# Attention: the first three score bursts of a batch moved beside the last three mixings of the batch in front of it, and added sums later in a slot

## The chip, the cores and the metric

The kernel runs on one core of one Trainium2 chip. Its time is the device time of one execution in microseconds (us). The kernel before took 1703.79 us (median of three runs, 1703.03 to 1704.57). Engines are named as the profile names them: PE multiplies matrices (PEld loads its weights), DVE is the vector engine, ACT the scalar engine, POOL the GpSimd engine, and SP the queue that starts most transfers.

## The reference, cut to what matters

The network has four layers on x of 8 batches, 512 positions and 256 columns: a state-space layer, a mixture of experts, attention and a second mixture of experts. Each layer is added to x and takes a layer norm of x as its input.

```python
def _L0_attn_b_ref(x, Wqkv, Wout):              # H = 16 heads of 16 columns
    qkv = jnp.einsum('btd,ed->bte', x, Wqkv)    # then cut into q, k, v by head
    scores = jnp.einsum('bhtd,bhsd->bhts', q, k) * SCALE
    scores = jnp.clip(scores, -10.0, 10.0)
    mask = jnp.triu(jnp.full((t, t), NEG), k=1)
    attn = jax.nn.softmax(scores + mask[None, None, :, :], axis=-1)
    out = jnp.einsum('bhts,bhsd->bhtd', attn, v)
    return jnp.einsum('btd,ed->bte', out.transpose(0, 2, 1, 3).reshape(b, t, d), Wout)

x = x + _L0_attn_a_ref(_layernorm(x), ...)      # state space
x = x + _L0_ffn_ref(_layernorm(x), ...)         # 16 routed experts, 4 for each token, and 2 shared ones
x = x + _L0_attn_b_ref(_layernorm(x), ...)
x = x + _L0_ffn_ref(_layernorm(x), ...)
```

## The kernel before

The work is done in stretches. The first holds the state-space layer. Then the routed experts of the first mixture run, which end near 722 us. The attention stage follows up to about 1190 us, and the routed experts of the second mixture are last. The change touches the attention stage, and lines below are those of the kernel before.

**A slot.** The attention stage runs over the eight batches. In slot b several pieces of work are issued beside each other: `main(b)`, the attention of batch b; `project(b + 1)`, the queries, keys and values of the next batch; the shared experts of batch b-2 (from slot 2 on); the routing of batch b-1 (norm, logits, choices) and the sends of rows of batch b-2 to their experts; and the loading and norm of x of batch b+2.

**How x arrives.** Each mixture's routed experts leave their results in two parts in memory. `load_sum` (L154) starts two transfers on SP for batch b+2, `more` from one part (L157) and x from the other (L158), and later DVE adds them in two steps of 128 x 512 numbers (L165). These two steps are kept where the program puts them in DVE's order. The statistics (L443, L444), the reciprocal deviation (L462, with a step of POOL at L463) and the normed rows (L468) of that batch follow.

**Projections.** `project` computes four results of 512 columns, pq_0_0, pq_0_1, pq_1_0 and pq_1_1 (first number: a half of the heads; second: queries or keys), each by PE at L1190 into a bank of a pool of four. Queries are copied by ACT (L1198). Keys are copied twice, by ACT (L1200) and by DVE (L1201), each time with every second head set to zero. Two results of values (pv, L1208) follow.

**Bursts and mixings.** `main` splits the scores of a half of the heads into five bursts, so that a batch has ten, named here 0_0 to 0_4 and 1_0 to 1_4. A burst (`weights`, L1228) is a group of score matmuls (L1238) into two banks of a pool that holds just two tiles of that size ("pair"), two exponentials on ACT (L1248, about 1.02 us each), and on DVE two pairs of clamps (L1258, L1259), which also apply the causal mask. Because scores can be clamped as well after the exponential, the limits are those of the exponential. A mixing (`mix`, L1264) multiplies the weights of a burst into the values (L1274). It stands LAG = 3 bursts behind its burst. After a half of the heads is mixed, `share` (L1286) turns the result, divides it by its sum and puts it into oT (L1289 to L1299); then the output projection (`add_projection`, L485) and the add to x (L494) end the batch.

`made` holds the weights of bursts, as pieces of a ring of ten tiles. The ring of queries and keys has six tiles. A column is what one matmul step costs in the pieces' own count.

**What sets the order.** `beside` (L348) issues steps of several pieces, always from the one that has done the smallest share of its columns; `timed` (L364) gives steps of a piece places in the slot between 0 and 1. A planner behind it then moves instructions within each engine's order, by its own costs, but keeps what is marked to stay. Each engine then takes its instructions in the order that comes out, and waits on semaphores.

In slots 2 to 6 (`close`), a burst and the mixing three bursts behind are issued as one step; in slots 0, 1 and 7 they are two steps.

Of the kernel before, what the change touches and what calls it, by code (L numbers as in the profile page):

```python
# [18 lines left out]
B, T, D = 8, 512, 256  # L19
NT = T // P  # L20
KD = D // P
# [57 lines left out]
LAG = 3  # L79
# [3 lines left out]
def tile_hybrid_block(  # L83
# [31 lines left out]
    def bank(shape, name: str, kind: str = "one"):  # L115
        kind = instead.get(kind, kind)
        return stage[kind].tile(shape, FP, tag=kind, name=name)
# [1044 lines left out]
    class Attention:  # L1162
        mixture, ahead, copies, turns = 1, 2, by_both, (0.65, 0.85)
        early = 2
        norms, scores, choose = (0.0, 0.12, 0.2, 0.28), (0.29, 0.45, 0.55, 0.6), (0.66, 0.95)
        last_rows, last_scores = (0.2, 0.28), (0.35, 0.38)

        def end(self):
            for e in range(first_expert, E):
# [5 lines left out]
        def project(self, b: int, xnT):  # L1175
            tag = f"a{b}"

            q_sb = spot("qk", NO)
            k_sb = [spot("qk", NO) for _ in range(2)]


            v_sb = values(f"v_{tag}").rearrange("p (t c) -> p t c", t=NT)

            def steps():
                nc.gpsimd.memset(v_sb, 1.0)
                for o in range(NO):
                    for which in range(2):
                        pq = bank([P, T], f"pq_{tag}_{o}_{which}")
                        for k in range(KD):
                            nc.tensor.matmul(  # L1190
                                pq,
                                lhsT=wqkv_sb[:, k, which * D + o * P : which * D + (o + 1) * P],
                                rhs=xnT[:, k, :],
                                start=(k == 0),
                                stop=(k == KD - 1),
                            )
                        if which == 0:
                            nc.scalar.copy(q_sb[:, o, :], pq)  # L1198
                        else:
                            nc.scalar.mul(k_sb[0][:, o, :], pq, parity[:, 0:1])  # L1200
                            nc.vector.tensor_scalar(k_sb[1][:, o, :], pq, parity[:, 1:2], None, ALU.mult)  # L1201
                        yield KD * T
                for h in range(2):
                    pv = bank([P, 2, D], f"pv_{tag}_{h}")
                    for j in range(2):
                        t = 2 * h + j
                        for k in range(KD):
                            nc.tensor.matmul(  # L1208
                                pv[:, j, :],
                                lhsT=xnT[:, k, t * P : (t + 1) * P],  # L1210
                                rhs=wqkv_sb[:, k, 2 * D : 3 * D],
                                start=(k == 0),
                                stop=(k == KD - 1),
                            )
                        nc.scalar.copy(
                            v_sb[:, t, 0 : H * VC].rearrange("p (h c) -> p h c", c=VC)[:, :, 0:DK],
                            pv[:, j, :].rearrange("p (h c) -> p h c", c=DK),
                        )
                        yield KD * D

            return (q_sb, k_sb, v_sb), Piece(2 * NO * KD * T + NT * KD * D, steps())

        def main(self, b: int, made):
            q_sb, k_sb, v_sb = made
            tag = f"a{b}"
            held = {}

            def weights(o: int, i: int, at):  # L1228


                ps = [bank([P, 2, T], f"ps_{tag}_{o}_{i}_{two}", "pair") for two in range(2)]
                es = [spot("es", 2) for _ in range(2)]
                col = 0
                for w, c in BANKS[i]:
                    n = T - c * P
                    for j in range(HG):
                        r = slice(32 * j, 32 * j + 32)
                        nc.tensor.matmul(  # L1238
                            ps[j // 2][:, j % 2, col : col + n],
                            lhsT=k_sb[w][r, o, c * P : (c + 1) * P],  # L1240
                            rhs=q_sb[r, o, c * P : T],
                            start=True,
                            stop=True,
                        )
                        at[w, c, j] = es[j // 2][:, j % 2, col : col + n]
                    col += n
                for two in range(2):
                    nc.scalar.activation(es[two], ps[two], AF.Exp, scale=ATT_SCALE)  # L1248
                    if len({w for w, _ in BANKS[i]}) > 1:
                        each = es[two].rearrange("p j (w q) -> p (j w) q", w=2)  # L1250
                        diagonal, full = each[:, :, 0:P], each[:, :, P:]
                        limit = causal[:, 0, :].unsqueeze(1).to_broadcast([P, 4, P])
                    else:
                        mixed = len(BANKS[i]) * P
                        diagonal, full = es[two][:, :, 0:mixed], es[two][:, :, mixed:]
                        limit = causal[:, 0 : len(BANKS[i]), :].rearrange("p c q -> p (c q)")
                        limit = limit.unsqueeze(1).to_broadcast([P, 2, mixed])
                    nc.vector.scalar_tensor_tensor(diagonal, diagonal, LOW, limit, ALU.max, ALU.min)  # L1258
                    nc.vector.tensor_scalar(full, full, LOW, TOP, ALU.max, ALU.min)  # L1259
                return len(BANKS[i]) * T  # L1260

            order = [key for keys in MIXES for key in keys]

            def mix(o: int, i: int, at):  # L1264


                ended = []
                for w, c in MIXES[i]:
                    places = [c for which, c in order if which == w]
                    if c == places[0]:  # L1270
                        at["po", w] = bank([P, T], f"po_{tag}_{o}_{w}")
                    for j in range(HG):
                        h = 8 * o + 2 * j + w
                        nc.tensor.matmul(  # L1274
                            at["po", w][32 * j : 32 * j + 32, c * P : T],
                            lhsT=v_sb[:, c, h * VC : h * VC + 32],
                            rhs=at[w, c, j],
                            start=(c == places[0]),
                            stop=(c == places[-1]),
                            tile_position=(0, 32 * j),  # L1280
                        )
                    if c == places[-1]:
                        ended.append(w)
                return len(MIXES[i]) * T, ended
# [15 lines left out]

            def steps():
                held["oT"] = work.tile([P, NO, T], FP, tag="kb4", name=f"oT_{tag}", bufs=KB)
                made = [{} for _ in range(NO)]
                bursts = [(o, i, made[o]) for o in range(NO) for i in range(len(BANKS))]

                close = 1 < b < B - 1
                for n in range(len(bursts) + LAG):
                    columns, ended = 0, []
                    if n < len(bursts):
                        columns = weights(*bursts[n])  # L1310
                        if n >= LAG and not close:
                            yield columns
                            columns = 0
                    if n >= LAG:
                        o, i, at = bursts[n - LAG]
                        more, ended = mix(o, i, at)
                        columns += more
                    yield columns
                    for w in ended:
                        share(o, w, at)  # L1320
                        yield 0
                yield from add_projection(b, lambda c: held["oT"][:, c, :], wo_sb, KD, tag)

            return Piece(2 * NO * 2 * NT * T + NT * KD * D, steps())


    ready = {}
# [47 lines left out]
    def stretch(layer):  # L1375
# [5 lines left out]
        def norm(b: int, first: bool = False):  # L1381
            def place():
                xn[b] = kb4(f"xn_{i}_{b}")
                return xn[b]

            return normed(b, f"l{i}_{b}", place, first, first)
# [52 lines left out]
        for b in range(1 if begun else 0, B):  # L1439
# [38 lines left out]
            if nxt < B:  # L1478
                added = layer.load(nxt)
                if added is not None:  # L1480
                    pieces.append(timed(added, 0.24, 0.28))
                pieces += [
                    timed(norm(nxt), *spread(0.32, 0.44, NT), *spread(0.56, 0.64, NT)),
                    timed(turn(nxt), *layer.turns),
                ]
            issue(beside(*pieces))
# [128 lines left out]
```

## Time and profile before

| what | us |
|---|---|
| median of three runs | 1703.79 |
| profiled execution | 1640.85 |
| its span | 1638.8 |
| PE busy in the span | 1572.8 (96%) |
| DVE busy | 1154.8 (70%) |
| ACT busy | 744.7 (45%) |
| POOL busy | 759.1 (46%) |
| PE busy / DVE busy, 828.2 to 888.9 us (slot 2) | 59.23 / 50.60 of 60.7 |

The profile is of one execution, with its time beside it; its span starts with the first and ends with the last instruction, and all places in us count from the span's start. A row of groups gives the line, the engine, the operation, what it writes and reads, the number of instructions, their busy time and the mean of one in ns, and the engine's idle time just before them with what ended it. A row of waits says which instruction an engine stood at, what released it, and how long in sum, how often, and at most. Durations of neighbouring instructions on one engine overlap a little in the records, by about 0.08 us, so that a sequence is shorter than the sum of its durations.

### The profile page before, as it was taken

How to read it: one execution, taken by the hardware profiler on the slowest of the kernel's cores; microseconds unless marked ns; L12 is line 12 of the kernel's file. 1: busy time of each engine (PE TensorE's matmuls, PEld its weight loads, DVE VectorE, ACT ScalarE, POOL GpSimd, SP SyncE). 2: the span in 40 equal slices, each digit the busy share in tenths (PEclk: the TensorE clock that was granted, in tenths of full speed). 3: DMA queues.
4: the chain of work that ended last, by engine and by line, in shares of the span. 5: the costliest groups of instructions: out<-in, count | busy, mean ns of one | idle time of the engine just before them, and what ended most of it. 6: DMA issues, size and time to landing. Idle time of an engine off the chain costs nothing.

```text
span 1638.8 us, 34229 instructions
## 1 busy us (share of the span) xinstructions
PE 1572.8 (96%) x9992; PEld 1156.9 (71%) x9992; DVE 1154.8 (70%) x3623; ACT 744.7 (45%) x1461; POOL 759.1 (46%) x655
## 2 busy tenths in 40 slices
PE   5999998999999999999899999999999999999996
PEld 2566665589999999974344445355458999999995
DVE  7988887546677666637887977977864666666664
ACT  3322332145555555545544444444314555555553
POOL 3265665635556555540022422422553555555554
PEclk8999999999999999999999999999999999999998
DMA  5355422557777766641324324332654777777776
GB/s 169 108 179 185 159 87 98 204 95 107 124 125 106 102 101 98 90 75 40 91 77 131 94 85 128 86 98 82 228 173 93 108 123 111 131 137 138 129 140 131
DMA packets 281646, 195.31 MB, mean 119 GB/s; under 512 B 168593, under 2 KB 262065, under 8 KB 281457
## 3 DMA queue, kind: packets, MB, share of 16 engines
q1 hardware_dynamic: 228368, 119.40, 28.8%
q0 software_dynamic: 51984, 72.09, 24.6%
q8 instruction: 85, 1.39, 0.4%
q10 hardware_dynamic: 1104, 1.57, 0.3%
q14 instruction: 105, 0.85, 0.2%
HBM read 89.71 MB, written 103.23 MB: 118 GB/s over the span
## 4 chain that ended last, share of the span: by engine, by line
PE 33%; DVE 11%; DMA 6%; issue 1%; ACT 1%; SPq 1%; POOL 1%; DVEq 0%; POOLq 0%; ACTq 0%
PE ph L993 12%; PE pyr L1024 6%; DMA part<-rows 4%; PE pg_m L1107 3%; PE pd_m L1136 3%; PE ps_a L1238 2%; DVE w_all L1258 2%; PE po_a L1274 2%; DVE w_all L1259 1%; PE py_a L485 1%; DMA x<-part 1%; PE pv_a L1208 1%; PE pq_a L1190 1%; ACT w_all L1248 1%; PE pt L975 1%
## 5 line engine op out<-in xcount | busy, mean ns | idle before, releaser
L1034 POOL DMA_INDIRECT part<-rows x272 | 426.8, 1569 | 339.4 <-ACT rows L1033 238.4
L758 POOL DMA_INDIRECT xg<-sorted_m,slots_m x256 | 257.9, 1007 | 244.3 <-issue 76.8
L993 PEld LDWEIGHTS ph<-rows,gate 128*128 128x128 f32 x2160 | 277.8, 191 | 33.4 <-ACT rows L976 23.2
L993 PE MATMUL ph<-rows,gate 128*128 128x128 f32 x2160 | 291.5, 278 | 1.8 <-ACT rows L976 1.8
L993 PE MATMUL ph<-rows,up 128*128 128x128 f32 x2160 | 285.3, 275 | 0.0
L1024 PE MATMUL pyr<-w_all,rows 128*128 x1088 | 279.2, 380 | 0.0
L966 DVE COPY up<-w_all 128x512 f32 x270 | 118.7, 441 | 211.9 <-PE ph L993 196.6
L993 PEld LDWEIGHTS ph<-rows,up 128*128 128x128 f32 x2160 | 262.9, 192 | 0.0
L966 ACT COPY gate<-w_all 128x512 f32 x270 | 166.5, 618 | 122.0 <-PE ph L993 116.3
L1024 PEld LDWEIGHTS pyr<-w_all,rows 128*128 128x128 f32 x1088 | 186.8, 192 | 14.3
L1248 ACT ACTIVATE w_all<-ps_a 128x1024 f32<-128x1024 f32 x160 | 155.1, 1021 | 69.8 <-PE ps_a L1238 59.8
L1033 ACT ACTIVATE rows<-pyr,gain 128x256 f32<-128x256 f32 x272 | 128.9, 474 | 80.9 <-PE pyr L1024 63.7
L1001 ACT ACTIVATE rows<-ph 128x256 f32<-128x256 f32 x272 | 104.6, 384 | 114.6 <-PE ph L993 99.7
L1003 DVE TENSOR_TENSOR rows<-ph,rows 128x256 f32<-128x256 f32 x272 | 115.0, 423 | 31.7 <-ACT rows L1001 31.6
L1004 DVE TENSOR_TENSOR rows<-ph,rows 128x256 f32<-128x256 f32 x272 | 115.2, 424 | 26.2 <-PE pt L975 0.9
L1107 PE MATMUL pg_m<-xT_m,su_sb 128*128 128x512 f32 x256 | 123.9, 605 | 0.0
L1136 PE MATMUL pd_m<-sd_sb,act_m 128*128 128x256 f32 x512 | 121.2, 382 | 1.3 <-DVE sig_m L1122 1.1
L1107 PE MATMUL pg_m<-xT_m,sg_sb 128*128 128x512 f32 x256 | 122.2, 600 | 0.0
L1238 PE MATMUL ps_a<-w_all 32*128 32x384 f32 (+3 forms) x1024 | 106.9, 473 | 8.7 <-ACT w_all L1248 8.6
L1136 PEld LDWEIGHTS pd_m<-sd_sb,act_m 128*128 128x128 f32 x512 | 95.8, 190 | 22.9 <-issue 7.0
L1258 DVE SCALAR_TENSOR_TENSOR w_all<-w_all,causal 128x512 f32<-128x512 f32 (+1 forms) x160 | 92.1, 575 | 17.9 <-ACT w_all L1248 17.5
L1238 PEld LDWEIGHTS ps_a<-w_all 32*128 32x128 f32 x1024 | 46.7, 188 | 68.6 <-ACT w_all L1248 43.6
(213 smaller groups left out, 1954.8 us busy)
## 6 DMA issues: line engine op xcount, KB each, us to landing
rows<-xg SPq DMA_DIRECT2D x720, 32.0 KB
rows<-xg SPq DMA_DIRECT2D x92, 134.0 KB
part<-x SPq DMA_DIRECT2D x16, 512.0 KB
part<-ys_m SPq DMA_DIRECT2D x14, 512.0 KB
sum<-part SPq DMA_DIRECT2D x14, 512.0 KB
w_all<-in_L_ffn_gate_w_dram SPq DMA_DIRECT2D x27, 256.0 KB
w_all<-in_L_ffn_up_w_dram SPq DMA_DIRECT2D x27, 256.0 KB
w_all<-in_L_ffn_down_w_dram SPq DMA_DIRECT2D x27, 256.0 KB
```

The source lines that it names most:

```text
L758: nc.gpsimd.indirect_dma_start(out=xg[i], out_offset=bass.IndirectOffsetOnAxis(ap=slots[:, at : at + 1], axis=0), in_=rows[:, t, :], in_of ...
L966: copy(here, w_all[:, bass.ds(held[n][0] + half * KD * F, KD * F)])
L993: nc.tensor.matmul(ph[s][:, f * P : (f + 1) * P], lhsT=both[s][:, k * F + f * P : k * F + (f + 1) * P], rhs=rows[:, ROW + k * P : ROW + (k ...
L1004: made = nc.vector.tensor_mul(act, ph[1], act)
L1024: nc.tensor.matmul(py, lhsT=act[:, f * P : (f + 1) * P], rhs=w_all[:, bass.ds(w + 2 * KD * F + f * D, D)], start=(f == 0), stop=(f == KF - 1),
L1033: nc.scalar.mul(y, py, gain[:, TK : TK + 1])
L1034: acc = nc.gpsimd.indirect_dma_start(out=parts[i][n % 2], out_offset=bass.IndirectOffsetOnAxis(ap=rows[:, D + 2 * TK : D + 2 * TK + 1].bit ...
L1107: made = nc.tensor.matmul(dst, lhsT=w[:, k, f * P : (f + 1) * P], rhs=xnT[:, k, :], start=(k == 0), stop=(k == KD - 1),)
L1136: nc.tensor.matmul(py[:, j, :], lhsT=acts[n][:, f, t * P : (t + 1) * P], rhs=shared[n][3][:, f, :], start=(n == 0 and f == 0), stop=(n == ...
L1238: nc.tensor.matmul(ps[j // 2][:, j % 2, col : col + n], lhsT=k_sb[w][r, o, c * P : (c + 1) * P], rhs=q_sb[r, o, c * P : T], start=True, st ...
L1248: nc.scalar.activation(es[two], ps[two], AF.Exp, scale=ATT_SCALE)
L1258: nc.vector.scalar_tensor_tensor(diagonal, diagonal, LOW, limit, ALU.max, ALU.min)
```

## The change

It has two parts.

1. The bursts of a batch are made known when it is projected (`bursts`, `parts`). `weights` takes the batch as an argument. The main work of batch b now goes over the ten mixings of b. Beside mixing n stands burst n + 3 of b, and beside the last three mixings stand the first three bursts of b+1. In slot 0 the first three bursts of batch 0 come ahead, so that slot 0 has thirteen bursts, slots 1 to 6 ten and slot 7 seven. A burst and a mixing are one step in every slot, so `close` goes. The piece's column count is corrected for slots 0 and 7.
2. The two steps of L165 stand at 0.31 and 0.34 of a slot, where they stood at 0.24 and 0.28. The statistics of that batch are spread from 0.36 to 0.44, where it was from 0.32 to 0.44. The state-space stage, which adds no parts, keeps 0.32.

```diff
         last_rows, last_scores = (0.2, 0.28), (0.35, 0.38)
+        bursts, parts = {}, {}
...
-            return (q_sb, k_sb, v_sb), Piece(2 * NO * KD * T + NT * KD * D, steps())
-
-        def main(self, b: int, made):
-            q_sb, k_sb, v_sb = made
+            each = [{} for _ in range(NO)]
+            self.bursts[b] = [(b, o, i, each[o]) for o in range(NO) for i in range(len(BANKS))]
+            self.parts[b] = q_sb, k_sb
+            return v_sb, Piece(2 * NO * KD * T + NT * KD * D, steps())
+
+        def main(self, b: int, v_sb):
...
-            def weights(o: int, i: int, at):
+            def weights(whose: int, o: int, i: int, at):
+                q_sb, k_sb = self.parts[whose]
+                tag = f"a{whose}"
...
             def steps():
                 held["oT"] = work.tile([P, NO, T], FP, tag="kb4", name=f"oT_{tag}", bufs=KB)
-                made = [{} for _ in range(NO)]
-                bursts = [(o, i, made[o]) for o in range(NO) for i in range(len(BANKS))]
-
-                close = 1 < b < B - 1
-                for n in range(len(bursts) + LAG):
-                    columns, ended = 0, []
-                    if n < len(bursts):
-                        columns = weights(*bursts[n])
-                        if n >= LAG and not close:
-                            yield columns
-                            columns = 0
-                    if n >= LAG:
-                        o, i, at = bursts[n - LAG]
-                        more, ended = mix(o, i, at)
-                        columns += more
-                    yield columns
+                many = len(self.bursts[b])
+                coming = iter([*(self.bursts[b] if b == 0 else self.bursts[b][LAG:]), *self.bursts.get(b + 1, [])[:LAG]])
+                if b == 0:
+                    for _ in range(LAG):
+                        yield weights(*next(coming))
+                for n in range(many):
+                    burst, columns = next(coming, None), 0
+                    if burst is not None:
+                        columns = weights(*burst)
+                    more, ended = mix(*self.bursts[b][n])
+                    yield columns + more
                     for w in ended:
-                        share(o, w, at)
+                        share(*self.bursts[b][n][1:2], w, self.bursts[b][n][3])
                         yield 0
                 yield from add_projection(b, lambda c: held["oT"][:, c, :], wo_sb, KD, tag)

-            return Piece(2 * NO * 2 * NT * T + NT * KD * D, steps())
+            more = (b == 0) - (b == B - 1)
+            columns = 2 * NO * 2 * NT * T + NT * KD * D + more * T * sum(len(keys) for keys in BANKS[:LAG])
+            return Piece(columns, steps())
...
                 if added is not None:
-                    pieces.append(timed(added, 0.24, 0.28))
+                    pieces.append(timed(added, 0.31, 0.34))
+                stats = 0.36 if added is not None else 0.32
                 pieces += [
-                    timed(norm(nxt), *spread(0.32, 0.44, NT), *spread(0.56, 0.64, NT)),
+                    timed(norm(nxt), *spread(stats, 0.44, NT), *spread(0.56, 0.64, NT)),
                     timed(turn(nxt), *layer.turns),
```

## The prediction

> **What bounds the kernel now.** I first read how busy each engine is in each slot of the attention stage (the stretch from one end of the output projection, L485, to the next; slot b mixes batch b). Columns: stretch, its length, busy time of PE, PEld, DVE, ACT, POOL (instructions), granted clock, DMA share, GB/s.
>
> ```profile
> core 0: us, PE busy (x) PEld busy (x) DVE busy (x) ACT busy (x) POOL busy (x), PEclk, DMA share, GB/s
> 734.20:779.10 44.90, 42.26 (x309) 18.84 (x308) 32.66 (x76) 24.88 (x30) 2.09 (x2) 0.96 0.18 48
> 779.10:828.20 49.10, 44.92 (x326) 20.00 (x325) 41.44 (x125) 23.51 (x29) 3.49 (x4) 0.93 0.29 76
> 828.20:888.90 60.70, 59.23 (x390) 29.09 (x390) 50.60 (x150) 27.63 (x43) 19.87 (x20) 1.00 0.32 98
> 950.40:1013.60 63.20, 59.30 (x393) 29.15 (x392) 50.36 (x147) 27.63 (x43) 19.92 (x20) 1.00 0.35 102
> 1076.90:1135.80 58.90, 58.90 (x393) 29.24 (x392) 45.37 (x130) 27.59 (x43) 17.30 (x18) 1.00 0.32 101
> 1135.80:1180.00 44.20, 40.62 (x314) 17.45 (x315) 40.06 (x128) 22.85 (x36) 17.72 (x18) 0.96 0.55 184
> ```
>
> Slot 6 lasts 58.90 us and PE is busy for all of it: slots 2 to 6 are bound by PE's work, and what slots 2 to 5 take beyond slot 6 (1.8, 2.6, 4.3, 4.4 us) is stall. Slots 0, 1 and 7 have less work. No matmul is added or removed, so only the stalls can change. Next, PE's waits between 734.2 and 1180 us (instruction waiting <- what released it: total us, times, longest).
>
> ```profile
> PE ps_a L1238 <- ACT w_all L1248: 8.6, 14, 2.6
> PE pq_a L1190 <- DVE w_all L1201: 8.5, 4, 3.4
> PE pr_m L707 <- DVE sel_m L699: 1.1, 1, 1.1
> PE pd_m L1136 <- DVE sig_m L1122: 1.1, 4, 0.4
> PE pv_a L1208 <- ACT v_a L1215: 0.7, 3, 0.2
> ```
>
> Two rows matter. The first is the chain burst, exponential, next burst in the same two-bank pool; its gaps lie in slots 0, 1 and 7 alone. The second is one gap in each of slots 2 to 5 (1.01, 1.79, 3.44, 2.25 us at 840.91, 902.43, 965.61, 1027.60): the fourth projection of a slot, pq_1_1, waits for its bank, which DVE's copy L1201 of pq_0_1 frees. Why L1201 is late stands in the rows of L165, the add of two parts:
>
> ```profile
> L165 DVE TENSOR_TENSOR x<-x,more x10: 682/688/692, 789.2 to 1026.2; 128x512 f32<-128x512 f32 x10
>   DMA x<-part: 16.5, 4
>   issue: 3.5, 1
> ```
>
> DVE takes its instructions in order. In slots 1 to 5 it stands 3.45 to 5.2 us before L165 for the load of x from part (at 899.49 the releaser is not resolved; the load went out at 894.74 there as elsewhere). With T the slot's start, that load goes out on SP behind the last row of L468 (T+5.4 to T+5.9) and lands at T+9.8, 10.6, 12.2, 11.1 in slots 2 to 5. DVE is at L165 at T+6 to T+8.5. So the chain is load, L165, L1201, pq_1_1.
>
> **Part 1: bursts moved.** Three bursts of b+1 (its score matmuls, two exponentials L1248, two clamp pairs L1258/L1259 each) go from the start of slot b+1 to the end of slot b, interleaved with mixings. They issue no DMA and nothing on POOL or SP; on PE they pass the output projection, on ACT two copies of shared results, on DVE the last transposes, the add L494 and the batch's statistics.
>
> *End of slots 1 to 6.* In the changed kernel's own instruction order the last mixing follows burst 2 of the next batch, and DVE has that burst's two clamp pairs ahead of the last transposes. After that burst's end t, PE has a mixing 1.07, shared down passes 4.0 and half an output projection 0.5, then wants oT at t+5.5. DVE: second exponential done at t+2.1, clamp pair 0.94, transpose 0.63, choice ops L691 and L699 0.76, reciprocal 0.17, product 0.34, transpose 0.61, together t+5.6, and some 0.3 of hand-overs: late by 0.4, bounds 0 and 1.0. The small waits on sig_m and v_a (0.23 each in most of these slots) find more cover, -0.4 per slot at best. Net about +0.1, five slots: **+0.5** (-2 to +4).
>
> *Slot 7.* Three bursts fewer; their 3.2 us of matmuls reappear in slot 6. Its chain stalls now, gaps and stretched matmuls together: 2.1 at 1138.7 to 1143.1, 1.1 at 1143.7, 1.06 at 1151.1, 1.07 at 1166.0, 5.3 in sum. With a mixing beside each burst from the start I keep about 2.3 of it. Choice is earlier by the same, which shortens the end (waits of 1.1 and 0.5, stretched matmuls about 1.3) by some 1.0. **-4.0** (-2 to -5.5).
>
> *Slots 0 and 1.* Slot 0 has thirteen bursts. The chain of the first ones, before any mixing, is unchanged; further stalls stay. Slot 1 loses 3.2 us of bursts and gains as many of the next batch's. Its DVE has 41.44 us of work, about 5 us of waiting for the load and 1.2 for POOL's rstd, so DVE rather than PE closes it at some 48.5, against 49.1; slot 0 grows by 3.2 for the bursts it takes and loses up to 2.2 of its stalls. The 2.6 us wait at ps_a, where ACT stands at a score behind DVE's logits, stays. **+0.5** (-1.5 to +2.5).
>
> **Part 2: sums later.** L165 goes from 0.24 to 0.31 of the slot, statistics of that batch to 0.36. But the slot's own list is shorter at its front by three bursts, and in the built order the first L165 stands behind the last row L468 and burst 3's clamp pairs, ahead of burst 4's. By PE's work ahead of it (burst 3 1.1, quarter mixing 0.5, projection 1.9) DVE reaches it at T+6 to T+7. The load's place on SP is the same, behind the same last row. So the wait remains. Behind it, ahead of L1201, stood one clamp pair and the second L165; now stand two clamp pairs, two statistics, two aggregates and, from slot 2 on, two row additions.
>
> Before, 899.49 to the end of L1201: 2.89 us. Steps from DVE's rows, each about 0.08 below its duration as neighbours overlap:
>
> ```profile
> L1258 DVE SCALAR_TENSOR_TENSOR w_all<-w_all,causal 128x512 f32<-128x512 f32 x48 | 32.8, 684 | 1.1 <-ACT w_all L1248 0.9
> L1259 DVE TENSOR_SCALAR w_all<-w_all 128x768 f32<-128x768 f32 x32 | 17.6, 550 | 0.0
> L1258 DVE SCALAR_TENSOR_TENSOR w_all<-w_all,causal 128x256 f32<-128x256 f32 x32 | 13.1, 410 | 0.2 <-ACT w_all L1248 0.2
> L1201 DVE TENSOR_SCALAR w_all<-pq_a,parity 128x512 f32<-128x512 f32 x8 | 5.9, 743 | 0.0
> ```
>
> After: L165 0.61 + clamp pairs 2 x 0.87 + statistics 0.66 + aggregates 0.25 + rows 0.2 + L1201 0.74 = 4.2 us, with small-step latencies 4.5. So L1201 ends 1.6 us later after the landing. PE wants pq_1_1 later too: burst 3 1.1, part of a mixing 0.5, pq 1.95, burst 4 1.15, mixing 1.0, pq 1.95, pr 0.8, pq 1.9, burst 1.1, mixing 0.85 put it at T+12.3, where it was T+11.75. Stalls: slot 3 10.6+4.5-12.3 = 2.8 (1.8 before), slot 4 4.4 (3.44), slot 5 3.3 (2.25): +3.0 in sum. In slot 2 only one clamp pair stands in between (about 3.4 us) and a part of burst 3 lies ahead of T, so the want is near T+11.6: 9.8+3.4-11.6 = 1.6, +0.5. **+3.5** (-8.5 if the load is home first, +6 if the additional work also runs late).
>
> **The clock.** A gap has a second price. These are stretches behind the gaps of slots 4 and 5, PE alone (length, PE busy, granted clock, DMA share):
>
> ```profile
> 965.60:969.00 3.40, 3.39 (x32) 1.00 0.00 0
> 1025.30:1027.60 2.30, 0.05 (x5) 1.00 0.57 77
> 1027.60:1031.00 3.40, 3.40 (x14) 0.64 0.00 0
> ```
>
> The 3.44 us gap cost no clock; the 2.25 us one was followed by 3.4 us at 0.64, and slot 5's PE busy time is 60.64 against 59.30 in slot 4: 1.3 us. The Trainium skill (TensorE: Matmul & The Clock Gate, HAM oscillation) puts the limit near 3.4 us of idleness, in a free-running window, and then half clock for about a window. It speaks against a change that lengthens gaps. By the rule only slot 4's new 4.4 us gap must pay, about 1.7 us (estimate: half of a 3.4 us window), and slot 5's 3.3 no longer, net +0.4. By the row, where one of four gaps paid and the longest did not, three longer gaps pay perhaps once or twice, +0 to +1.3 over before. I take **+0.7** (-1.3 to +2.7).
>
> **Sum**: +0.5 - 4.0 + 0.5 + 3.5 + 0.7 = +1.2 us on the profiled execution (1640.85 us, span 1638.8 and 2.05 around it), which becomes 1642.05. The runs' median lies 62.9 above the profiled execution, and I carry the difference over unchanged: 1703.8 + 1.2 = **1705.0 us**.
>
> **Rivals.** *A, slower: the clamp backlog becomes every slot's bound.* Place: the two clamp pairs ahead of the last transposes, and those ahead of L1201. It decides when DVE reaches either over 0.3 us later than I put it; for then every excess goes straight to PE, which has nothing else in its order: 8 x 0.3 = 2.4, and 1707.4. At 0.6 us in both places in slots 2 to 5, and 1.3 us of clock in two of them more: +1.2 + 8 x 0.6 + 2.6 = +8.6, or 1712. For it: DVE is 50 of 61 us busy and loses 4 at one wait. Against: 10 us of slack remain over the whole slot.
>
> *B, faster: the added load is home before DVE gets there.* If L165 really falls 0.07 of 61 us = 4.3 us later, at T+11.3, it meets landings at T+9.8 to 12.2. The gaps go, -8.5, and slot 5's clock, -1.3; with slot 7 -4.0, ends +0.5 and slots 0 and 1 +0.5 that is -12.8: 1691, or 1695 if half of the gaps go. Against: the built order puts L165 ahead of burst 4's clamps.
>
> *C, the ends gain and the middle doesn't lose.* The backlog of 1.6 us finds cover as PE's list is late itself: +0.5 - 4.0 + 0.5 + 0 = -3.0, 1700.8. The change doing nothing of what it says in the middle is this case.
>
> **How the numbers follow.** A measurement of this kernel can tell about 0.2% (3.4 us) from no change: the bounds are 1700.4 and 1707.2. Forecast 0.42 (own range 1701 to 1709: 0.33 within, 0.09 slower), A 0.28 (slower), B 0.17 (faster), C 0.13 (0.05 faster, 0.08 within). Faster 0.22, same 0.41, slower 0.37. The range 1698 to 1712 leaves out B and the upper end of A.
>
> **What would show it.** Right: in slots 3 to 5 DVE still waits at L165 for the load, now with two clamp pairs and statistics between it and the copy of k (L1201's successor), and pq_1_1's gaps are longer by about 1 us each; ps_a's waits in slot 7 fall from three stalls to two; the last output projection of slots 2 to 6 shows a new wait of under 1 us on the transpose. Wrong: L165 without a wait and pq_1_1 without a gap (B); waits of over 1.5 us at L485 (A). A different landing time of the load, from other DMA traffic, would upset the sum most, microsecond for microsecond in four slots.

## The result, and the profile after

The changed kernel takes 1705.80 us (median of 20 runs, 1700.66 to 1711.86), the kernel before 1701.22 (20 runs, 1695.92 to 1706.91): a ratio of 1.0032, 95% interval 1.0022 to 1.0043, so 3.7 to 7.3 us slower. The profiled execution of after took 1710.02 us (span 1708.3).

The profiled execution of before that the prediction used (1640.85 us) lies 55 us below the fastest timed run of this result, so it was most likely made on a faster chip. Outside the attention stage its span and that of after differ by some 40 us, in stages that the change leaves alone. I therefore compare slots, not spans, and took both kernels' profiles again on chips of the faster kind. The record numbers the chips of the later runs: two on which before takes about 1644 us, which I call A1 and A2, and one on which it takes 1701.26, which I call B. It does not number the chip of the result. Before takes 1701.22 there, and the profile of after has the long waits of B, so I count it as B.

Line numbers of the changed kernel are one to five higher than before's from L1190 on.

PE's waits in the attention stage of after (749 to 1250 us), the same view as before's:

```profile
PE pq_a L1191 <- DVE w_all L1202: 13.4, 4, 4.1
PE ps_a L1243 <- ACT w_all L1253: 11.5, 11, 4.3
PE py_a L485 <- DVE oT_a L1304: 9.8, 7, 1.8
PE pd_m L1136 <- DVE act_m L1123: 2.2, 4, 0.6
```

The gap at pq_a is still there in four slots, and has grown from 8.5 to 13.4 us. Two rows are new. The output projection waits for the last transpose (oT) in every slot but the last: 1.75 us in each of slots 2 to 5. A down pass of the shared experts, a step of PE that reads a product of DVE (act_m), waits 0.6 us in the same slots.

The slots (same columns as before: length, PE, PEld, DVE, ACT, POOL, clock, DMA, GB/s), from slot 2 on:

```profile
861.55:926.39 64.84, 60.58 (x389) 29.30 (x388) 49.85 (x149) 26.85 (x42) 19.66 (x20) 0.97 0.30 92
...
994.20:1061.92 67.72, 61.81 (x392) 29.76 (x392) 50.18 (x147) 27.76 (x43) 19.43 (x20) 0.95 0.32 95
...
1128.43:1187.77 59.34, 58.63 (x393) 28.92 (x392) 45.42 (x130) 27.88 (x43) 18.06 (x18) 1.00 0.32 100
1187.77:1240.49 52.72, 46.83 (x296) 20.37 (x296) 38.95 (x127) 17.70 (x33) 20.11 (x21) 0.94 0.56 184
```

Slot 2 has 4.1 us more than in the first profile of before, slot 4 4.5 us, slot 6 only 0.4. DVE's work is the same; PE's busy time in slot 4 is 61.81 us at a clock of 0.95, where about as many matmuls take 58.63 in slot 6 at 1.00.

The add L165 in after:

```profile
L165 DVE TENSOR_TENSOR x<-x,more x16: 678/683/693, 494.2 to 1091.2; 128x512 f32<-128x512 f32 x16
...
  DMA x<-part: 17.1, 4
  issue: 5.2, 1
```

In slots 1 to 5 DVE stands before it for 22.3 us in sum, about as long as it did (16.5 and 3.5 us before). In slot 3 (start at 926.39) it waits from 932.55 to 937.78, and the copy L1202 ends at 942.22, 4.44 us later; before, that stretch was 2.89.

### The profile page after: what moved, and what is told of

Read it like the earlier page. It is cut to its first block, busy times and chain, and to the rows that moved or that the text cites. A ratio compares the mean times of both kernels' runs of the same rounds, so it can differ in the third digit from the quotient of the medians.

```text
span 1708.3 us, 34231 instructions
## 1 busy us (share of the span) xinstructions
PE 1588.3 (93%) x9992; PEld 1161.0 (68%) x9992; DVE 1153.2 (68%) x3623; ACT 745.1 (44%) x1461; POOL 755.5 (44%) x655
## 5 line engine op out<-in xcount | busy, mean ns | idle before, releaser
L993 PEld LDWEIGHTS ph<-rows,gate 128*128 128x128 f32 x2160 | 277.8, 191 | 33.3 <-ACT rows L976 22.5
L993 PE MATMUL ph<-rows,gate 128*128 128x128 f32 x2160 | 291.5, 278 | 1.8 <-ACT rows L976 1.8
L993 PE MATMUL ph<-rows,up 128*128 128x128 f32 x2160 | 285.3, 275 | 0.0
L993 PEld LDWEIGHTS ph<-rows,up 128*128 128x128 f32 x2160 | 262.9, 192 | 0.0
L1243 PE MATMUL ps_a<-w_all 32*128 32x384 f32 (+3 forms) x1024 | 110.9, 484 | 11.8 <-ACT w_all L1253 11.5
```

Source lines behind the costliest of these rows:

```text
L993: nc.tensor.matmul(ph[s][:, f * P : (f + 1) * P], lhsT=both[s][:, k * F + f * P : k * F + (f + 1) * P], rhs=rows[:, ROW + k * P : ROW + (k ...
L1243: nc.tensor.matmul(ps[j // 2][:, j % 2, col : col + n], lhsT=k_sb[w][r, o, c * P : (c + 1) * P], rhs=q_sb[r, o, c * P : T], start=True, st ...
```

## The experiments

All times are medians of device us, each compared with runs of the kernel before on the same chip: 1645.34 on A1, 1643.43 on A2, 1701.26 on B. Runs on different chips are compared by these ratios.

**Before, profiled again** (no edit).

> The kernel before, once more, for a profile on the chip of these runs. The profiled execution of before took 1640.85 us, its timed runs about 1701. If the profile of the changed kernel (1710.02) differs from the first profile of before by more than the change, by about 60 us in stages that the change leaves alone, this one should lie near 1700 us, with the long waits before the experts' tables (L870, about 11 us twice) and at a route's sums (L707, about 15 us) that the changed kernel's profile shows. If those waits belong to the change, they are absent here and the time is near 1640.

Measured on A1: one execution of 1652.79 us, with no long wait at L870. By the letter of the expectation the long waits would belong to the change; but the changed kernel, profiled on A2 below, has none either (0.6 us at L870), and on B all four variants and the changed kernel have one of 10 to 12. They go with the chip. What this profile does tell is that before itself varies: its waits at pq_a add up to 12.3 us here, 8.5 in the first profile. The timed runs of before on A1 lie between 1640.83 and 1649.60, so the first profile is of an execution at their lower end and this one is above them all.

```profile
PE pq_a L1190 <- DVE w_all L1201: 12.3, 4, 4.4
PE ps_a L1238 <- ACT w_all L1248: 8.5, 12, 3.2
```

**Part 2 alone** (on A1).

```diff
-                    pieces.append(timed(added, 0.24, 0.28))
+                    pieces.append(timed(added, 0.31, 0.34))
+                stats = 0.36 if added is not None else 0.32
-                    timed(norm(nxt), *spread(0.32, 0.44, NT), ...
+                    timed(norm(nxt), *spread(stats, 0.44, NT), ...
```

> Part 2 alone: bursts as before, sums at 0.31 and 0.34. In this kernel's own order the first add L165 stands behind the copy L1201 of pq_0_1 in slots 2 to 5, so nothing that PE waits for stands behind the load. Theory (the add's place ahead of the copy sets the middle of slots 2 to 5): the four gaps of pq_a (8.5 us before) are gone, with up to 1.3 us of clock; 7 to 11 us faster than before, about 1692. Rival (the load's wait moves to the next thing behind the add, clamps and mixings): the gaps turn up at po_a or ps_a and the gain stays under 3 us.

Measured: 1639.34 us, ratio 0.9961 (0.9946 to 0.9977), 6.0 us faster. The mechanism held; the size fell short of the 7 to 11 us expected.

```profile
PE ps_a L1238 <- ACT w_all L1248: 9.0, 14, 3.1
PE pd_m L1136 <- DVE sig_m L1122: 6.6, 4, 1.7
```

No row of pq_a is left. In its place PE waits up to 1.7 us for sig_m, a product of DVE for the shared experts, at the end of slots 2 to 5: DVE's work now stands later in the slot, and some 5 us of the gain goes there (6.6 us against 1.4 in the profile above). Slots 2 to 5 take 60.8 us each.

**Part 1 alone** (the changed kernel with 0.24, 0.28 and 0.32 again; on A1).

> Part 1 alone: bursts moved, sums at 0.24 and 0.28. From slot 2 on its order on DVE up to the second copy of keys is that of the changed kernel. Theory (with the bursts moved the later place changes nothing in slots 2 to 5): as the changed kernel within 2 us, 4 to 7 us slower than before; pq_a gaps of about 13 us in sum. Rival (part 2 is what costs, by a later norm and turn): within 2 us of before.

Measured: 1656.41 us, ratio 1.0071 (1.0054 to 1.0087), 11 us slower. The loss is larger than the 4 to 7 us expected. Its waits at pq_a are 12.9 us, those of oT 9.3.

**The changed kernel beside the other variants** (no edit).

> The changed kernel once more, timed beside the other variants on one chip. Part 1 alone was 0.71% slower than before on the chip of those runs. Theory (with the bursts moved, the later place of the sums changes nothing from slot 2 on): 0.5 to 0.8% slower than before here as well, slots 3 to 5 about 65 to 68 us. Rival (the later sums win back a part): 0.2 to 0.4% slower.

Measured on A2: 1655.39 us, ratio 1.0077 (1.0059 to 1.0096), where part 1 alone has 1.0071 on A1. So with the bursts moved, the later place of the sums does nothing that these intervals, of about 0.2% either way, could show: the theory holds. Part 1 takes away the effect of part 2, because a slot's own burst 3, not burst 0, is now at its front, and in DVE's order the add stays ahead of the copy that PE wants. On A2 the change costs more than twice what it costs in the result.

```profile
PE pq_a L1191 <- DVE w_all L1202: 12.6, 4, 3.7
PE py_a L485 <- DVE oT_a L1304: 9.8, 7, 1.8
```

Slot by slot (from the last output projection of one slot to that of the next; slot 0 from the last matmul of L993, which belongs to the routed experts), on A1, the changed kernel on A2, one profiled execution each:

| us | slot 0 | 1 | 2 | 3 | 4 | 5 | 6 | 7 |
|---|---|---|---|---|---|---|---|---|
| before, again | 59.38 | 50.00 | 60.94 | 63.48 | 66.48 | 65.80 | 58.87 | 53.23 |
| sums alone | 58.70 | 51.42 | 60.76 | 60.76 | 60.81 | 60.81 | 58.87 | 52.88 |
| bursts alone | 65.46 | 50.10 | 63.83 | 67.17 | 65.35 | 65.65 | 59.33 | 44.26 |
| changed | 63.93 | 50.49 | 63.16 | 64.50 | 67.54 | 67.86 | 59.33 | 47.18 |

**Sums later still, behind the copy** (the changed kernel with this edit; on A1). The statistics end at 0.52 in place of 0.44, and rows of the next batch go from 0.56-0.64 to 0.58-0.66.

```diff
-                    pieces.append(timed(added, 0.31, 0.34))
-                stats = 0.36 if added is not None else 0.32
+                    pieces.append(timed(added, 0.42, 0.45))
+                stats = 0.46 if added is not None else 0.32
```

> The changed kernel with the sums at 0.42 and 0.45, statistics of that batch from 0.46 to 0.52 and rows from 0.58 to 0.66: the add stands behind the copy of pq_0_1 in slots 2 to 5. Theory (the stretch of DVE's work between load and copy is what the changed kernel lost by): the pq_a gaps (13.4 us in the changed kernel's profile) are gone, 11 to 15 us faster than the changed kernel and so 6 to 10 us faster than before. Rival (the loss is at the slots' ends, where the output projection waits for the last transpose, and in slots 0 and 7): within 4 us of the changed kernel.

Measured: 1662.76 us, ratio 1.0104 (1.0086 to 1.0122): slower than part 1 alone, on the same chip, by 6.4 us. My theory in this form fell. The gaps at pq_a did go, as it said, and all that they gave was taken elsewhere:

```profile
PE py_a L485 <- DVE oT_a L1304: 13.4, 7, 3.7
PE ps_a L1243 <- ACT w_all L1253: 10.9, 16, 3.6
PE pg_m L1107 <- DVE act_m L1123: 5.2, 4, 1.3
PE pd_m L1136 <- DVE act_m L1123: 5.1, 5, 1.2
```

Slots 2 to 5 are 64.1 us each, and slot 0 is 70.9. So there is a second cause at the end of a slot, and it grows as other work of DVE is put off.

**Mixing ahead of the next batch's burst** (the changed kernel with this edit; on A2).

```diff
                     burst, columns = next(coming, None), 0
-                    if burst is not None:
+                    first = burst is not None and burst[0] == b
+                    if first:
                         columns = weights(*burst)
...
+                    if burst is not None and not first:
+                        yield weights(*burst)
```

> The changed kernel with one edit: beside the last three mixings of a batch the next batch's burst is issued after the mixing, not before it, so that on DVE the last transposes stand ahead of the clamps of burst 2 of the next batch. Theory (clamps ahead of the transposes delay the output projection by 1.2 to 1.8 us in a slot, and that is most of what slots 1 to 6 lose beyond the gap at pq_a): the waits of py_a on oT, 9 to 10 us in sum, fall below 3, and the time is 5 to 8 us below the changed kernel. Rival (DVE is late as a whole; the clamps passed by come due at once in the next slot's first mixings and at the copy of keys): the waits at py_a go, those at pq_a, po_a or ps_a grow by as much, within 2 us of the changed kernel.

Measured: 1661.27 us, ratio 1.0108 (1.0091 to 1.0125), 5.9 us slower than the changed kernel. The theory, that it is the order of clamps and transposes, is refuted. In slots 2 to 5 (840 to 1110 us) the wait at oT has gone, and one of about the same size stands at act_m, 1.7 us in each. In slots 0 and 1 the wait at oT has grown from 0.8 and 1.3 us to 2.8 and 5.7:

```profile
PE pq_a L1191 <- DVE w_all L1202: 13.1, 4, 3.7
PE pd_m L1136 <- DVE act_m L1123: 6.6, 4, 1.7
...
PE py_a L485 <- DVE oT_a L1304: 8.5, 2, 5.7
```

The last row is from all slots. The rival was right that DVE is late as a whole, though it named another place for the wait and at most 2 us for the time.

**Both: mixing first, sums at 0.42** (on A2).

> Mixing ahead of the next batch's burst, as in the run before, and the sums at 0.42 and 0.45, so that neither the load's wait nor the moved clamps stand ahead of what PE wants. Theory (two causes, each of which PE sees): no gaps at pq_a, under 3 us at py_a, slots 2 to 5 at 61 to 62 us; 10 to 15 us faster than the changed kernel, 4 us or more faster than before. Rival (with the sums at 0.42 DVE has too much left at a slot's end whatever the order, as the run with bursts before mixings had, 1.04% slower): slots 2 to 5 stay near 64 us, slower than before.

Measured: 1651.19 us, ratio 1.0055 (1.0036 to 1.0075): 4.2 us below the changed kernel, still slower than before. Slots 2 to 5 stay at 63.6 to 63.7, as the rival said; PE waits 3.0 to 4.5 us in each for act_m. None of the orders tried of the same work frees a slot's end.

**The move at the last boundary only**, with sums at 0.31 and 0.34 (the changed kernel with this edit; on A2).

```diff
-                coming = iter([*(self.bursts[b] if b == 0 else self.bursts[b][LAG:]), *self.bursts.get(b + 1, [])[:LAG]])
-                if b == 0:
+                own = self.bursts[b][LAG:] if b in moved else self.bursts[b]
+                coming = iter([*own, *(self.bursts[b + 1][:LAG] if b + 1 in moved else [])])
+                if b not in moved:
                     for _ in range(LAG):
                         yield weights(*next(coming))
...
+                        if b < 2:
+                            yield columns
+                            columns = 0
...
-            more = (b == 0) - (b == B - 1)
+            more = (b + 1 in moved) - (b in moved)
```

Here `moved` holds batch 7 alone.

> Sums at 0.31 and 0.34, and bursts moved at one boundary only: the first three bursts of batch 7 beside the last three mixings of batch 6; all other slots issue their bursts as before. Theory (the move pays where slot 7 is short of work, and costs in slots that are full): slot 6 longer by 3.2 to 4 us, slot 7 shorter by 7 to 9, slots 0 to 5 as with the sums alone; 4 to 6 us faster than the sums alone, so about 0.65% faster than before. Rival (slot 7's gain in part 1 came from the slots in front of it): within 1 us of the sums alone, 0.3 to 0.45% faster than before.

Measured: 1642.04 us, ratio 0.9989 (0.9979 to 0.9999), where the sums alone have 0.9961 on A1: some 4.6 us slower than these by the ratios. Neither side was right. Slot 7 falls from 52.88 to 45.62 us as the theory said, but slot 6, now with thirteen bursts, grows from 58.87 to 69.02: 10.2 us for 3.2 us of matmuls. A down pass of its shared experts stands 2.7 us at act_m, and after that gap the clock was low (columns: stretch, length, PE, PEld, DVE, ACT, POOL, clock, DMA, GB/s):

```profile
1120.00:1130.00 10.00, 7.32 (x53) 3.77 (x56) 8.29 (x34) 2.62 (x4) 4.13 (x4) 0.97 0.15 55
1130.00:1141.50 11.50, 11.50 (x68) 8.54 (x64) 5.64 (x13) 3.11 (x4) 0.00 (x0) 0.88 0.08 24
```

The clock was at half for 3.4 us, from 1129.44 on, which costs 1.7 us; 2.5 of the 10.2 us stay unexplained. Slot 0 of the changed kernel also takes three bursts without giving three away, and it too grows by more than their matmuls, 4.6 us.

The last group ran on B. As before takes the same time there as in the result, its times are set beside the 1705.80 us of the changed kernel.

**Less work at a slot's end.** Leaves out the limits on the keys off the diagonal in bursts 0_0 to 0_2 of every batch.

```diff
-                    nc.vector.tensor_scalar(full, full, LOW, TOP, ALU.max, ALU.min)
+                    if o or i >= LAG:
+                        nc.vector.tensor_scalar(full, full, LOW, TOP, ALU.max, ALU.min)
```

> The changed kernel, leaving out the limits L1264 on the keys off the diagonal in the first three bursts of every batch, the ones that part 1 moves: six instructions, about 2.7 us of DVE's work, less in each slot. Theory (DVE is late as a whole at a slot's end, as the moved clamps come on top of the shared experts and the choice): PE's waits for oT and act_m in slots 2 to 5, 1.8 and 0.6 us in each, fall under 0.5 together; pq_a's gaps stay at 12 to 14 us in sum; 6 to 9 us below the changed kernel. Rival (order, not amount: what stands ahead of the transposes decides): the waits fall by at most the clamps directly ahead, 0.9 us in a slot, under 4 us in all.

Measured: 1692.45 us, ratio to before 0.9947 (0.9928 to 0.9967), 13.4 us below the changed kernel, more than the theory asked. Waits for oT fall to 0.1 us a slot and those for act_m vanish. In slots 0 to 7 the rows of PE's waits on DVE that are left are those at pq_a and two of under 1 us:

```profile
PE pq_a L1191 <- DVE w_all L1202: 14.6, 4, 4.2
PE ps_a L1243 <- ACT w_all L1253: 12.2, 11, 5.0
```

At a slot's end it is the amount of DVE's work that counts, not its order.

**The second copy of keys on ACT**, so that PE no longer depends on DVE for that bank.

```diff
-                            nc.vector.tensor_scalar(k_sb[1][:, o, :], pq, parity[:, 1:2], None, ALU.mult)
+                            nc.scalar.mul(k_sb[1][:, o, :], pq, parity[:, 1:2])
```

> The changed kernel with the second copy of keys (L1202) on ACT in place of DVE, two instructions in a slot of about 0.7 us each. Theory (PE meets the load's wait only through that copy): pq_a's gaps (12.6 us in sum, with 2.5 us of clock[...]) are gone and nothing takes their place before the slot's end; waits at oT and act_m stay near 2.4 us in a slot; 12 to 18 us below the changed kernel, so 0 to 5 us below before. Rival (behind the load stand clamps as well; the next mixing of their bursts waits): gaps of 1 to 3 us in each slot at po_a, under 8 us gained.

Measured: 1693.82 us, ratio 0.9963 (0.9943 to 0.9982), 12.0 us below the changed kernel, at the theory's lower end.

```profile
PE py_a L485 <- DVE oT_a L1304: 9.8, 7, 1.8
PE pv_a L1209 <- DVE tr_a L1294: 3.5, 3, 1.2
PE pd_m L1136 <- DVE act_m L1123: 2.2, 4, 0.6
PE po_a L1279 <- DVE where_m L715: 1.8, 3, 0.7
```

The row of pq_a is gone. The theory had nothing in its place; 5.3 us of smaller waits for DVE stand there, some at po_a, as the rival said. The waits at oT and act_m are as in the changed kernel, to the tenth, though DVE has two copies less to do in each slot: what is taken from a slot's start does not help its end.

**Both edits.**

> Both edits at once: keys on ACT, and the limits L1264 left out in the first three bursts of every batch. Theory (two separate causes in slots 2 to 5): the gains add, slots 2 to 5 at 58.8 to 59.5 us, 20 to 25 us below the changed kernel and 8 to 12 below before. Rival (one cause, DVE's total work): the second edit brings under 3 us over the first.

Measured: 1681.79 us, ratio 0.9890 (0.9868 to 0.9911), 24.0 us below the changed kernel, where the two alone add up to 25.3. The causes are separate. Slots 2 to 5 are at 59.7, 61.1, 60.7 and 60.5 us, a little above the 58.8 to 59.5 expected, for the small waits just named (0.7 to 2.1 us a slot) stay:

```profile
PE pv_a L1209 <- DVE tr_a L1295: 4.2, 4, 1.2
PE po_a L1280 <- DVE where_m L715: 1.8, 3, 0.9
```

**The sums alone, with keys on ACT**: the second copy of keys on ACT, in the kernel with part 2 alone.

> A candidate for a faster kernel: bursts as before, sums at 0.31 and 0.34 (0.39% faster than before on this chip type of run), and the second copy of keys on ACT. Theory: the wait on sig_m at a slot's end (1.6 us in slots 2 to 5), the last one left there, falls as DVE has 1.3 us less to do in each slot; slots 2 to 5 at 59.0 to 60.0; 3 to 7 us below the sums alone, 0.55 to 0.8% below before. Rival (ACT is late by the copies and PE waits for it at pq or pv): as the sums alone or slower.

Measured: 1685.35 us, ratio 0.9912 (0.9894 to 0.9931): 15.9 us faster than before and 20.5 below the changed kernel, the fastest kernel that computes all. But its theory failed: the wait on sig_m is what it was,

```profile
PE ps_a L1238 <- ACT w_all L1248: 9.3, 15, 2.4
PE pd_m L1136 <- DVE sig_m L1122: 6.6, 4, 1.7
```

and slots 2 to 5 are at 60.8, as with the sums alone. As that one was timed on A1 only, whether the copy on ACT adds anything to it stays open; the slots speak for nothing or little.

## Why the prediction was right or wrong

The forecast was 1705.0 us in 1698 to 1712, and 1705.80 was measured. So close a hit is luck. The forecast put +1.2 us on 1703.8, the median of before's first three runs; the longer series has 1701.22, and the change itself cost 4.6 us by the medians, 5.4 by the ratio. Several terms are off, in both directions. The prediction had named its own sign of being wrong at a slot's end: a wait at L485 of under 1 us would speak for it, one of over 1.5 us for rival A. The waits are 1.75 us in slots 2 to 5. So there the mechanism is rival A's, at one of the two places that A names; at the other, ahead of the copy of keys, DVE was not late.

*The chain load, L165, copy of keys, pq_1_1: right.* DVE still stands at the add, and from there to the end of the copy it takes 4.44 us against the 4.5 worked out. Forecast gaps in slots 2 to 5: 1.6, 2.8, 4.4, 3.3, together 12.1 us; measured 1.9, 4.1, 3.6, 3.8 in the profile of the result (13.4) and 1.9, 3.2, 3.7, 3.7 on A2 (12.6). That the sums agree is again luck in part. PE wants pq_1_1 at T+11.8 in slots 3 to 5, as before, not at T+12.3, and the load in slot 4 landed at T+10.9, not at T+12.2. The comparison was weak too: before's own gaps vary with the landing of the load, 8.5 us in the profile used and 12.3 in the second one, where DVE begins the add at T+13.2 and T+13.0 in slots 4 and 5. The term's +3.5 was a difference to a favourable execution.

*End of slots 1 to 6: mis-sized, and this is the step that failed.* +0.5 was forecast, with 0.4 us late at oT and up to 0.4 won back. Measured are 1.8 us at oT and 0.6 at act_m in each of slots 2 to 5, 1.3 in slot 1 and 0.7 in slot 6. Against some 0.4 us of such waits in before that is about +2.0 in each of slots 2 to 5, and with slot 6 +8.7, over the bound of +4 (slot 1 is counted below). The error is in DVE's chain after the last moved burst. With t at the burst's end, the prediction let one of its two clamp pairs run beside the second exponential and so had oT ready at t+5.9. This is part 1 alone, slot 3, where the burst ends at 952.34:

```profile
951.19 1.15 PE L1243 MATMUL ps_a<-w_all 32*128 32x256 f32 x16
952.43 1.94 ACT L1253 ACTIVATE w_all<-ps_a 128x1024 f32<-128x1024 f32 x2 [2.25 <-PE ps_a L1243]
953.03 0.68 DVE L1122 SCALAR_TENSOR_TENSOR sig_m<-sig_m,pg_m 128x512 f32<-128x512 f32 x1
953.81 0.69 DVE L1123 SCALAR_TENSOR_TENSOR act_m<-sig_m,pg_m 128x512 f32<-128x512 f32 x1
954.42 0.69 DVE L1263 SCALAR_TENSOR_TENSOR w_all<-w_all,causal 128x512 f32<-128x512 f32 x1
...
958.29 0.71 DVE L1304 STREAM_TRANSPOSE oT_a<-tr_a 128x512 f32<-128x512 f32 x1
959.06 0.70 PE L485 MATMUL py_a<-w_att,oT_a 128*128 128x256 f32 x2 [1.64 <-DVE oT_a L1304]
```

DVE had come in without a pause and was still at a shared expert's products (L1122, L1123), which the prediction's list left out. The first clamp pair began only at t+2.1 and the second behind it, so one pair, 0.9 us, came on top, and PE went on with oT at t+6.7. PE itself was ready at t+5.1 in place of t+5.5. The two differences make the 1.2 us between 0.4 and 1.6. The experiments show that it is the amount of work there: leaving out half of the moved clamps takes the whole wait away, another order of the same work moves it to act_m, and less work at the slot's start leaves it as it was.

DVE is 50 of 61 us busy in before, but its free time lies at both ends of a slot. In slot 4 of before, profiled again, DVE has these busy times in the first and the last 14 us:

```profile
953.74:967.74 14.00, 6.56 (x18) 1.00 0.65 189
1006.22:1020.22 14.00, 8.45 (x19) 1.00 0.08 29
```

Of 15.8 us without work 7.4 lie at the start, where DVE stands for the load, and 5.5 at the end, most of them behind the last transpose, where it waits for PE's projection. Between them lie 2.8, in 38 us. Part 1 took clamps from the start and put them ahead of the last transposes, into the full stretch.

*Sums later: right.* The reading of the built order, that the add stays ahead of the copy, is confirmed: the changed kernel and part 1 alone agree. Rival B's mechanism is real where the order allows it: part 2 alone removes the gaps and gains 6.0 us.

*The clock: mis-sized.* I took +0.7, with 1.3 us for a gap. Around the gap of slot 3 in after (columns: stretch, length, PE, clock, DMA share, GB/s):

```profile
938.17:940.52 2.35, 0.01 (x1) 1.00 0.52 67
940.52:942.27 1.75, 0.00 (x0) 0.50 0.00 0
942.27:947.34 5.07, 5.07 (x20) 0.50 0.00 0
947.34:955.00 7.66, 7.66 (x73) 1.00 0.20 73
```

The clock goes to half while PE still stands, 2.35 us into a gap of 4.10, and stays there for 6.8 us. PE works in 5.07 of these and loses 2.5. Against 58.95 us of PE's busy time in a slot at full clock, slots 2 to 5 of after have 60.6, 61.4, 61.8 and 60.4, together 8.4 us more. The changed kernel on A2 has 5.5 more in slots 4 and 5 (61.5 and 61.8; gaps of 3.70 and 3.72 us) and nothing in slots 2 and 3 (gaps of 1.90 and 3.23). Before had 1.4 us of this in the first profile, but 5.7 in the second. The row that I weighed higher in the prediction was cut off the clock's own steps: its 0.64 is full clock until 1028.55 and half for the 3.4 us after. The Trainium skill's rule (TensorE: Matmul & The Clock Gate, HAM oscillation; a limit near 3.4 us) did better: in the profiles here all 15 gaps of 3.45 us or more in slots 2 to 6 lost clock. Yet gaps of 1.95 us in after, 2.25 in before and 2.7 in the run with the last boundary alone did so too, and the rule does not explain these.

*Slot 7: right.* -4.0 forecast. With 3.24 us for the three bursts that went to slot 6, the last boundary alone gives 52.88 - 45.62 - 3.24 = 4.0, the changed kernel on A2 2.8, part 1 alone 5.7. *Slots 0 and 1:* +0.5 forecast, +1.8 measured on A2 (4.55 - 3.24 in slot 0, 0.5 in slot 1), with the new wait at oT in both.

Rival C fell: its sum kept +0.5 for the slots' ends, where +8.7 was measured. Its middle without a loss holds for pq_a against the second profile of before (12.6 us against 12.3), but not against the first.

What stays open is the different size of the loss, 0.32% in the result and 0.77% on A2. There is no profile of before on B. The sums alone with keys on ACT gain 15.9 us there, the sums alone 6.0 on A1, with equal slots 2 to 5. If the copy on ACT adds nothing to the sums, before loses more at its gaps on B than on A1, and the change had less to add; no run shows it. Open too is how much of the loss of 12.0 us on A2 lies where. Against the slow second profile of before the eight slots of the table are 5.8 us longer in sum, and a profile of before at its median is missing.

## What to carry to other kernels

Before moving work of an engine that isn't the bound to another place, look when in a loop it is idle, not how much: here DVE's free 10 us of 61 lay at both ends of the slot, and work moved from its start to just ahead of the last transpose became PE's wait. Where PE hangs on a bank, ask what else stands in the queue of the engine that frees it; moving one short copy to an engine without such a wait ahead of it was worth 12 us in the changed kernel, though DVE stood for the load as before. One edit may undo another: test each alone, since here part 2 gained 6 us and part 1 took that gain away.

## What the runs showed of the hardware

The granted clock of PE in slots 2 to 6 of all fourteen profiles: each of 15 gaps of 3.45 us or more was followed by, or already held, a stretch at half clock, of 3.4 us in eight cases and 6.8 in seven. Of 16 gaps from 1.87 to 3.44 us ten had one, of 3.4 us, and of 53 gaps from 1.0 to 1.8 us two. So no sharp limit shows, and a gap of 3.44 us cost nothing where one of 1.87 did.

In slots 1 to 5 of both profiles of before and of three with the bursts moved (part 1 alone, the changed kernel twice) DVE stood 2.9 to 6.1 us for one load, with ready clamps and copies behind it in its order, and PE stood up to 4.4 us for one of these copies.

The same kernel takes 1645 and 1643 us on two chips and 1701 on a third. The attention stage is a part of it, but the stretch from the start to the first routed experts alone is 27 us longer (370.2 against 343.3 us for the changed kernel), and the stretch between attention and the second routed experts 13.5 (71.9 against 58.4). There DVE has single waits of up to about 11 us that the trace doesn't resolve. What causes those was not tried.
